# Transposing the inner layers of two routed expert blocks together, in three pieces

## The chip, the cores and the metric

The kernel runs on one core of a Trainium2 chip. A core has a matrix engine (TensorE, PE in the profile; its weight loads are shown apart as PEld), a vector engine (VectorE, DVE), a scalar engine (ScalarE, ACT), a general engine (GpSimd, POOL) and an engine that mostly issues transfers (SyncE, SP). Each has its own queue of instructions, taken in order; semaphores tie them together. Operands lie in an on-chip memory of 128 partitions; the matrix engine writes to a second, smaller one (PSUM), from which DVE and ACT copy. The metric is the device time of one execution, in microseconds (us). Twelve runs of the kernel before gave a median of 989.9 us, from 986.58 to 996.82 us.

## The reference

All arithmetic is in 32-bit floats. The input is x, 8 sequences of 256 tokens with 256 features (2048 tokens). Three residual layers follow one another:

```python
x = x + 0.5 * ffn(layernorm(x))      # mixture of experts
x = x + attention(layernorm(x))      # 16 heads, each query looks at its 32 best keys
x = x + 0.5 * ffn(layernorm(x))      # the same weights again

# ffn, for one token t with its 2 best of 8 experts:
scores = softmax(t @ gate_w)
routed = sum over the 2 experts e of
         scores[e] * (silu(t @ w_gate[e]) * (t @ w_up[e])) @ w_down[e]
shared = (silu(t @ sw_gate) * (t @ sw_up)) @ sw_down
out    = routed + shared
```

An expert's inner layer has 176 units, the shared one's 352. The change concerns the routed part only, which is computed in both feed-forward layers.

## The kernel before

**Routing.** Tokens are sorted by expert into blocks of 128 slots, so that all the tokens of one block use one expert. A block's tokens are fetched by an indirect transfer from a copy of the normalised tokens in DRAM, and its results are stored by an indirect transfer to `y_dram`; both are issued by POOL (L520 and L591). With 2048 tokens, two experts each and 8 experts, 37 blocks are always computed (`ND`), and two more only in a rare distribution, behind a branch (`rare`).

**A block.** Block b goes through these parts, in functions of these names:

- `fetch` (L520): 128 tokens come into tile `xs`, one token per partition.
- `turn` (L531, L533): two transposes on PE into PSUM (`px`), and one ACT copy into `xsT`.
- `widen` (L543 to L555): matmuls of `xsT` with the expert's gate and up weights give `pgu` (2 x 176 columns); ACT takes the silu (`sl`, L553), DVE multiplies it with the other half, and the inner layer `h` (128 tokens x 176 units, L555) is done. In the first pass a weight load for the attention is issued behind it.
- `turn_hidden` (L563, L565): the 176 units must come to the partitions for the next matmul. They are cut into two halves of 88: two PE transposes of 128 x 88 go into PSUM (`ph`), and one DVE copy of 88 partitions x 256 brings both to `hT`.
- `narrow` (L571 to L591): two accumulating matmuls over 88 units each, with 256 columns of `w_down`, give `py`. DVE works out the token's weight `ws` (L580), ACT multiplies (`y`, L589), POOL stores.

A matmul in 32-bit floats shows as two records in the profile, a transpose as one.

**Order.** `routed` runs over steps. In step s, PE does `widen(s)`, `turn(s+2)`, `turn_hidden(s-2)` and `narrow(s-4)`, so that each part was prepared one or more steps ago by ACT or DVE. A scheduler puts the instructions of each engine in order by their dependencies; PE keeps the order of the steps. PSUM has two buffers of each kind: `pgu`, `px`, `ph` and `py` can each be at most two blocks ahead of the engine that empties them. In SBUF, `xs` has 13 buffers (8 fetches are issued ahead), `xsT`, `h` and `hT` have 4 each and `y` has 8. POOL's queue holds fetches and stores alternately.

**Weights.** The eight experts' weights lie in one tile `wall`, a row of columns per expert; the two halves of `w_down` lie in partitions 0 to 87 in two column ranges. The expert for a block is chosen at run time by a column offset held in a register of PE (`locate`). The loads are issued by SP (L121) in the first layer's normalisation.

**Around it.** Ahead of the blocks stand the layer norm, the shared expert's first half and the routing; after them the shared expert of the remaining seven tiles, and then, in the first pass, the attention, in the second, the sum with the stored results (`yg`, L638; DVE L644) and the output.

Of the kernel before, what the change touches and what calls it, by code (L numbers as in the profile page):

```python
# [8 lines left out]
F32 = mybir.dt.float32  # L9
# [3 lines left out]
ALU = mybir.AluOpType  # L13
AX = mybir.AxisListType

P = 128
# [7 lines left out]
def macaron_kernel(  # L24
# [19 lines left out]
    nc = tc.nc  # L44

    B, S, D = x_in.shape
    NT = B * S // P
    KD = D // P
# [5 lines left out]
    E, _, HE = w_gate.shape  # L54
    HS = sw_gate.shape[1]
    K = 2
    assert E == 8 and HS == 2 * HE and HE % 2 == 0
    HH = HE // 2
    NSC = (HS + P - 1) // P


# [1 line left out]
    ND = (NT * P * K) // P + E // 2 + 1  # L63
# [18 lines left out]
    psum = ctx.enter_context(tc.tile_pool(name="psum", bufs=2, space=bass.MemoryType.PSUM))  # L82
# [12 lines left out]
    wall = wts.tile([P, E, EW], F32, name="wall")  # L95
# [24 lines left out]
    def later(loads, out, in_, queue=nc.sync):  # L120
        loads.append(lambda: queue.dma_start(out=out, in_=in_))  # L121

    for k in range(KD):
        for j, w in ((0, w_gate), (1, w_up)):
            c0 = (2 * k + j) * HE
# [4 lines left out]
            )  # L130
    for c in range(2):
        c0 = 2 * KD * HE + c * D
        later(
            expert_loads,
            wall[0:HH, :, c0 : c0 + D],
            w_down[:, c * HH : (c + 1) * HH, :].rearrange("e h d -> h e d"),
        )
    later(attn_loads, wi_sb[:, :, HI, :], wk_idx.rearrange("(k p) d -> p k d", p=P))
    later(attn_loads, wk_sb, wk.rearrange("(k p) d -> p k d", p=P))
# [18 lines left out]
    ident = const.tile([P, P], F32, name="ident")  # L158
# [287 lines left out]
    def ffn(n, pool, block_pool, ahead):  # L446
# [65 lines left out]
            nc.vector.scalar_tensor_tensor(x[:, i, :], po, 0.5, x[:, i, :], ALU.mult, ALU.add)  # L512

        w = wall.rearrange("p e c -> p (e c)")
        xs, xsT, hT, turned, c0 = {}, {}, {}, {}, {}

        def fetch(b, slot_pool):

            xs[b] = slot_pool.tile([P, DR], F32, tag="xs", name=f"xs_{n}_{b}", bufs=XB + XH)
            nc.gpsimd.indirect_dma_start(  # L520
                out=xs[b],
                out_offset=None,
                in_=xn_dram,
                in_offset=bass.IndirectOffsetOnAxis(ap=token[:, b : b + 1], axis=0),
            )

        def turn(b):

            px = psum.tile([P, KD, P], F32, tag="B", name=f"px_{n}_{b}")
            for k in range(KD):  # L530
                nc.tensor.transpose(px[:, k, :], xs[b][:, k * P : (k + 1) * P], ident)  # L531
            xsT[b] = block_pool.tile([P, KD, P], F32, tag="xsT", name=f"xsT_{n}_{b}", bufs=4)
            nc.scalar.copy(xsT[b], px)  # L533

        def locate(b):

            c0[b] = nc.tensor.value_load(cols[0:1, b : b + 1], min_val=0, max_val=(E - 1) * EW)

        def widen(b):

            pgu = psum.tile([P, 2, HE], F32, tag="A", name=f"pgu_{n}_{b}")
            for k in range(KD):
                nc.tensor.matmul(  # L543
                    pgu,
                    xsT[b][:, k, :],
                    w[:, bass.ds(c0[b] + 2 * k * HE, 2 * HE)],
                    start=(k == 0),
                    stop=(k == KD - 1),
                )
            if b + 1 < ND:  # L550
                locate(b + 1)
            sl = block_pool.tile([P, HE], F32, tag="sl", name=f"sl_{n}_{b}", bufs=3)
            nc.scalar.activation(sl, pgu[:, 0, :], AF.Silu)  # L553
            h = block_pool.tile([P, HE], F32, tag="h", name=f"h_{n}_{b}", bufs=4)
            scaled = nc.vector.tensor_tensor(h, sl, pgu[:, 1, :], ALU.mult)  # L555
            if attn_loads:
                behind(attn_loads.pop(0)(), scaled, "spread over the blocks")
            return h

        def turn_hidden(b, h):  # L560
            ph = psum.tile([HH, 2, P], F32, tag="C", name=f"ph_{n}_{b}")
            for c in range(2):
                nc.tensor.transpose(ph[:, c, :], h[:, c * HH : (c + 1) * HH], ident)  # L563
            hT[b] = block_pool.tile([HH, 2, P], F32, tag="hT", name=f"hT_{n}_{b}", bufs=4)
            turned[b] = nc.vector.tensor_copy(hT[b], ph)  # L565

        def narrow(b, slot_pool):

            py = psum.tile([P, D], F32, tag="D", name=f"py_{n}_{b}")
            for c in range(2):  # L570
                nc.tensor.matmul(  # L571
                    py,
                    hT[b][:, c, :],
                    w[0:HH, bass.ds(c0[b] + 2 * KD * HE + c * D, D)],
                    start=(c == 0),
                    stop=(c == 1),
                )
            ws = block_pool.tile([P, 1], F32, tag="ws", name=f"ws_{n}_{b}", bufs=4)
            with tc.issue_after(turned[b].ins):
                nc.vector.scalar_tensor_tensor(  # L580
                    ws,
                    xs[b][:, D + 1 : D + 2],
                    choice[:, b : b + 1],
                    xs[b][:, D : D + 1],
                    ALU.mult,
                    ALU.add,
                )
            y = slot_pool.tile([P, D], F32, tag="y", name=f"y_{n}_{b}", bufs=SB)
            nc.scalar.mul(y, py, ws)  # L589

            stored = nc.gpsimd.indirect_dma_start(  # L591
                out=y_dram,
                out_offset=bass.IndirectOffsetOnAxis(ap=dest[:, b : b + 1], axis=0),
                in_=y,
                in_offset=None,
            ).ins
            tc.declare_no_dep(stored, group=f"y_{n}", reason="rows that differ")
            tc.add_to_no_dep_group(f"y_{n}", stored)

        def routed(slot_pool):  # L600


            for b in range(XB):
                fetch(b, slot_pool)
            locate(0)
            turn(0)
            turn(1)
            h = {}
            for b in range(ND + 4):
                if b < ND:  # L610
                    h[b] = widen(b)
                if b + 2 < ND:
                    turn(b + 2)
                if 2 <= b < ND + 2:
                    turn_hidden(b - 2, h[b - 2])
                if b >= 4:
                    narrow(b - 4, slot_pool)
                if b + XB < ND:
                    fetch(b + XB, slot_pool)

        def rare(count, slot_pool):

            with tc.If(count > ND):
                for b in range(ND, NB):
                    fetch(b, slot_pool)
                    locate(b)
                    turn(b)
                    turn_hidden(b, widen(b))
                    narrow(b, slot_pool)

        parts = y_dram[NT * P * K : 2 * NT * P * K, :].rearrange("(i p k) d -> p i k d", k=K, p=P)
# [60 lines left out]
    igroups, c0 = [], 0  # L692
# [477 lines left out]
```

## Time and profile before

| | |
|---|---|
| median of 12 runs | 989.9 us |
| profiled execution, its own time | 990.67 us |
| span of the profiled execution | 988.7 us |
| mean granted TensorE clock | 0.987 |
| PE busy | 929.9 us (94%) |
| DVE busy | 513.2 us (52%) |
| ACT busy | 403.8 us (41%) |
| POOL busy | 305.8 us (31%) |
| first block's first matmul, first pass / second pass | at 68.05 / 848.45 us |
| last block's last matmuls begin, first pass / second pass | at 178.06 / 958.81 us |

The span runs from the first instruction to the last. A group is named by its line, its engine and its tiles ("ph<-ident,h" is written by a transpose of `h`), with the number of its instructions, its busy time and the mean time of one. A matmul's time covers its way through the array, so that a following one begins before it ends; what a matmul costs in a stream is read from the distance between starts.

### The profile page before, as it was taken

How to read it: one execution, taken by the hardware profiler on the slowest of the kernel's cores; microseconds unless marked ns; L12 is line 12 of the kernel's file. 1: busy time of each engine (PE TensorE's matmuls, PEld its weight loads, DVE VectorE, ACT ScalarE, POOL GpSimd, SP SyncE). 2: the span in 40 equal slices, each digit the busy share in tenths (PEclk: the TensorE clock that was granted, in tenths of full speed). 3: DMA queues.
4: the chain of work that ended last, by engine and by line, in shares of the span. 5: the costliest groups of instructions: out<-in, count | busy, mean ns of one | idle time of the engine just before them, and what ended most of it. 6: DMA issues, size and time to landing. Idle time of an engine off the chain costs nothing. (4 is left out here: it accounts for less than half of the span.)

```text
span 988.7 us, 16072 instructions
## 1 busy us (share of the span) xinstructions
PE 929.9 (94%) x4412; PEld 740.6 (75%) x4412; DVE 513.2 (52%) x1986; ACT 403.8 (41%) x1297; POOL 305.8 (31%) x501
## 2 busy tenths in 40 slices
PE   6998989999999999999999999999988999798898
PEld 3665667689878888888888888888867667566675
DVE  5442233594757566475464665565566527222236
ACT  4422333234554445435435435435434442233331
POOL 2035664300132232222222223223234400566640
PEclk9997999999999999999999999999999999999899
DMA  9324532342152433333243243233244610222217
GB/s 304 91 55 134 179 115 76 112 141 78 45 169 79 131 120 102 99 127 114 75 139 114 88 140 106 98 111 113 100 123 138 202 38 7 76 86 88 89 63 262
DMA packets 124158, 111.98 MB, mean 113 GB/s; under 512 B 32326, under 2 KB 106022, under 8 KB 124070
## 3 DMA queue, kind: packets, MB, share of 16 engines
q1 hardware_dynamic: 107078, 63.30, 22.3%
q0 software_dynamic: 14272, 45.18, 13.1%
q10 hardware_dynamic: 2720, 2.47, 0.8%
q8 instruction: 38, 0.62, 0.3%
q14 instruction: 50, 0.41, 0.1%
HBM read 63.97 MB, written 46.92 MB: 112 GB/s over the span
## 5 line engine op out<-in xcount | busy, mean ns | idle before, releaser
L945 POOL TENSOR_TENSOR s<-s,rden 128x512 f32<-128x512 f32 (+1 forms) x60 | 87.8, 1464 | 180.8 <-DVE rden L944 176.4
L543 PE MATMUL pgu<-wall,xsT 128*128 x296 | 106.1, 482 | 19.8 <-ACT xsT L533 10.5
L520 POOL DMA_INDIRECT xs<-xn_dram,token x74 | 71.3, 963 | 163.3 <-DVE dest L425 114.0
L935 ACT ACTIVATE s<-s,anm 128x32 f32<-128x32 f32 (+1 forms) x240 | 96.5, 404 | 54.1 <-DVE anm L931 19.1
L997 PE MATMUL pwo<-wo_sb,oT 128*128 128x256 f32 x512 | 116.9, 380 | 1.4 <-ACT oT L978 1.4
L676 PE MATMUL pqT<-xnT,wq_sb 128*128 128x256 f32 x512 | 116.7, 379 | 0.7 <-ACT qT L726 0.7
L997 PEld LDWEIGHTS pwo<-wo_sb,oT 128*128 128x128 f32 x512 | 96.4, 190 | 26.8 <-issue 9.1
L676 PEld LDWEIGHTS pqT<-xnT,wq_sb 128*128 128x128 f32 x512 | 96.8, 190 | 13.2 <-ACT qT L726 1.1
L676 PE MATMUL pqi<-xnT,wi_sb 128*128 128x224 f32 x512 | 103.3, 353 | 0.0
L555 DVE TENSOR_TENSOR h<-sl,pgu 128x176 f32<-128x176 f32 x74 | 24.9, 337 | 137.7 <-ACT sl L553 94.9
L676 PEld LDWEIGHTS pqi<-xnT,wi_sb 128*128 128x128 f32 x512 | 95.7, 190 | 0.8
L911 PE MATMUL ps<-kT,qT 128*128 128x160 f32 (+7 forms) x512 | 86.0, 310 | 7.7 <-DVE amx L920 4.6
L911 PEld LDWEIGHTS ps<-kT,qT 128*128 128x128 f32 x512 | 75.5, 191 | 21.3 <-ACT r L815 9.5
L543 PEld LDWEIGHTS pgu<-wall,xsT 128*128 128x128 f32 x296 | 56.5, 195 | 44.5 <-ACT xsT L533 16.6
L971 PE MATMUL pav<-s,v 128*128 128x512 f32 x180 | 87.9, 592 | 0.0
L591 POOL DMA_INDIRECT y_dram<-y,dest x74 | 71.8, 971 | 50.4 <-ACT y L589 28.7
L571 PE MATMUL py<-wall,hT 88*128 x296 | 78.3, 390 | 8.3 <-ACT y L589 8.3
L952 DVE STREAM_TRANSPOSE sq<-s 128x512 f32<-128x512 f32 (+1 forms) x60 | 58.5, 975 | 52.0 <-POOL s L945 52.0
L920 DVE CUSTOM_DVE_ANT_0 s<-ps,bias 128x32 f32<-128x32 f32 (+1 forms) x240 | 61.8, 300 | 42.4 <-PE ps L911 23.0
L800 DVE SCALAR_TENSOR_TENSOR acc<-r,iwp,acc 128x96 f32<-128x96 f32 x168 | 74.9, 499 | 13.7 <-ACT r L815 13.7
L978 ACT COPY oT<-pav 128x512 f32<-128x512 f32 x64 | 37.3, 583 | 69.7 <-PE pav L971 69.4
L589 ACT ACTIVATE y<-py,ws 128x256 f32<-128x256 f32 x74 | 35.3, 478 | 72.5 <-PE py L571 37.6
(171 smaller groups left out, 1450.8 us busy)
## 6 DMA issues: line engine op xcount, KB each, us to landing
s<-sq_dram SPq DMA_DIRECT2D x360, 64.0 KB
sq_dram<-sq POOLq DMA_DIRECT2D x32, 512.0 KB
sq_dram<-sq POOLq DMA_DIRECT2D x32, 256.0 KB
yg<-y_dram SPq DMA_DIRECT2D x18, 256.0 KB
xn_dram<-xn SPq DMA_DIRECT2D x32, 128.0 KB
yg<-y_dram SPq DMA_DIRECT2D x7, 512.0 KB
acc_dram<-acc SPq DMA_DIRECT2D x8, 368.0 KB
wi_sb<-in_L_attn_wq_idx_dram SPq DMA_DIRECT2D x8, 256.0 KB
```

The source lines that it names most:

```text
L520: nc.gpsimd.indirect_dma_start(out=xs[b], out_offset=None, in_=xn_dram, in_offset=bass.IndirectOffsetOnAxis(ap=token[:, b : b + 1], axis=0),)
L543: nc.tensor.matmul(pgu, xsT[b][:, k, :], w[:, bass.ds(c0[b] + 2 * k * HE, 2 * HE)], start=(k == 0), stop=(k == KD - 1),)
L571: nc.tensor.matmul(py, hT[b][:, c, :], w[0:HH, bass.ds(c0[b] + 2 * KD * HE + c * D, D)], start=(c == 0), stop=(c == 1),)
L591: stored = nc.gpsimd.indirect_dma_start(out=y_dram, out_offset=bass.IndirectOffsetOnAxis(ap=dest[:, b : b + 1], axis=0), in_=y, in_offset= ...
L676: nc.tensor.matmul(ps[:, j, :], weights(k, h0 + hh + j), xnT[:, k, b * S + skip : (b + 1) * S], start=(k == 0), stop=(k == KD - 1),)
L800: nc.vector.scalar_tensor_tensor(acc[:, cols], r, iw, acc[:, cols], ALU.mult, ALU.add)
L911: nc.tensor.matmul(ps[:, c0 - first : c0 - first + n], qT[:, t * NQ + q].rearrange("p h k -> p (h k)"), kT[:, 0:n], start=True, stop=True,)
L920: nc.vector.tensor_tensor_reduce(out=s[:, q, 0:n], in0=ps[:, c0 - first : c0 - first + n], in1=bias[t][:, c0 : c0 + n], scale=1.0, scalar= ...
L935: nc.scalar.activation(scores, scores, AF.Exp, bias=nm[:, q : q + 1], scale=SCALE, accum_out=den[:, q : q + 1],)
L945: nc.gpsimd.tensor_tensor(s, s, rden.unsqueeze(2).to_broadcast([P, NQ, ns]), ALU.mult)
L971: nc.tensor.matmul(po.rearrange("p h r -> p (h r)"), v[:, c, 0:HD], pT[:, c].rearrange("p h r -> p (h r)"), start=(c == 0), stop=(c == t),)
L997: nc.tensor.matmul(po, oT[:, h, :], wo_sb[:, w0 + h, :], start=(h == 0), stop=(h == HW - 1),)
```

## The change

The inner layer is cut into 112 and 64 units instead of 88 and 88, and two blocks share one tile `h` of 352 columns: first the 112 and the 64 of the even block, then the 64 and the 112 of the odd one, so that the two pieces of 64 lie side by side. The even block's multiplication stays one DVE instruction, the odd one's becomes two. Every second step, three transposes serve two blocks: one of 112 columns for each, and one of 128 columns that holds both pieces of 64; they land in partitions 0 to 63 and 64 to 127. DVE then copies each block's 112 partitions and its 64 partitions, 128 columns each, four copies for two blocks, where there were two of 256 columns. The second matmul of `narrow` works on 64 partitions. `narrow` runs five steps after `widen` instead of four; the tile `h` has 3 buffers of double width, `hT` 5. The 37th block has no partner and is turned alone, with two transposes. The load of `w_down` is cut at 112.

```diff
-    HH = HE // 2
+    HT = P // 2
+    HM = HE - HT
...
-            wall[0:HH, :, c0 : c0 + D],
-            w_down[:, c * HH : (c + 1) * HH, :].rearrange("e h d -> h e d"),
+            wall[0:n, :, c0 : c0 + D],
+            w_down[:, h0 : h0 + n, :].rearrange("e h d -> h e d"),
...
-            h = block_pool.tile([P, HE], F32, tag="h", name=f"h_{n}_{b}", bufs=4)
-            scaled = nc.vector.tensor_tensor(h, sl, pgu[:, 1, :], ALU.mult)
+            if j == 0:
+                hs[b] = hs[b + 1] = block_pool.tile(
+                    [P, 2 * HE], F32, tag="h", name=f"h_{n}_{b}", bufs=3
+                )
+            for lo, hi, to in ((0, HE, 0),) if j == 0 else ((HM, HE, HE), (0, HM, HE + HT)):
+                scaled = nc.vector.tensor_tensor(
+                    hs[b][:, to : to + hi - lo], sl[:, lo:hi], pgu[:, 1, lo:hi], ALU.mult
+                )
...
-            ph = psum.tile([HH, 2, P], F32, tag="C", name=f"ph_{n}_{b}")
-            for c in range(2):
-                nc.tensor.transpose(ph[:, c, :], h[:, c * HH : (c + 1) * HH], ident)
-            hT[b] = block_pool.tile([HH, 2, P], F32, tag="hT", name=f"hT_{n}_{b}", bufs=4)
-            turned[b] = nc.vector.tensor_copy(hT[b], ph)
+            b, m = blocks[0], len(blocks)
+            ph = psum.tile([P, 3, P], F32, tag="C", name=f"ph_{n}_{b}")
+            for j in range(m):
+                to = j * (HE + HT)
+                nc.tensor.transpose(ph[0:HM, j, :], hs[b][:, to : to + HM], ident)
+            nc.tensor.transpose(ph[0 : m * HT, 2, :], hs[b][:, HM : HM + m * HT], ident)
+            for j in range(m):
+                hT[b + j] = block_pool.tile([P, 2, P], F32, tag="hT", name=f"hT_{n}_{b + j}", bufs=5)
+                nc.vector.tensor_copy(hT[b + j][0:HM, 0, :], ph[0:HM, j, :])
+                turned[b + j] = nc.vector.tensor_copy(
+                    hT[b + j][0:HT, 1, :], ph[j * HT : (j + 1) * HT, 2, :]
+                )
...
             for c in range(2):
+                rows = (HM, HT)[c]
                 nc.tensor.matmul(
                     py,
-                    hT[b][:, c, :],
-                    w[0:HH, bass.ds(c0[b] + 2 * KD * HE + c * D, D)],
+                    hT[b][0:rows, c, :],
+                    w[0:rows, bass.ds(c0[b] + 2 * KD * HE + c * D, D)],
...
-            for b in range(ND + 4):
+            for b in range(ND + 5):
                 if b < ND:
-                    h[b] = widen(b)
+                    widen(b, b % 2)
                 if b + 2 < ND:
                     turn(b + 2)
-                if 2 <= b < ND + 2:
-                    turn_hidden(b - 2, h[b - 2])
-                if b >= 4:
-                    narrow(b - 4, slot_pool)
+                if b % 2 and b >= 3 and b - 3 < ND:
+                    turn_hidden(range(b - 3, min(b - 1, ND)))
+                if b >= 5:
+                    narrow(b - 5, slot_pool)
```

More of the change, by code (lines that the diff above doesn't have):

```diff
@@ L56, in macaron_kernel @@
     K = 2
-    assert E == 8 and HS == 2 * HE and HE % 2 == 0
-    HH = HE // 2
+    assert E == 8 and HS == 2 * HE and P // 2 < HE <= P + P // 2
+    HT = P // 2
+    HM = HE - HT
     NSC = (HS + P - 1) // P
@@ L132, in macaron_kernel @@
         c0 = 2 * KD * HE + c * D
+        h0, n = c * HM, (HM, HT)[c]
         later(
             expert_loads,
-            wall[0:HH, :, c0 : c0 + D],
-            w_down[:, c * HH : (c + 1) * HH, :].rearrange("e h d -> h e d"),
+            wall[0:n, :, c0 : c0 + D],
+            w_down[:, h0 : h0 + n, :].rearrange("e h d -> h e d"),
         )
@@ L514, in ffn @@
         w = wall.rearrange("p e c -> p (e c)")
-        xs, xsT, hT, turned, c0 = {}, {}, {}, {}, {}
+        xs, xsT, hs, hT, turned, c0 = {}, {}, {}, {}, {}, {}
         def fetch(b, slot_pool):
@@ L537, in locate, with widen @@
             c0[b] = nc.tensor.value_load(cols[0:1, b : b + 1], min_val=0, max_val=(E - 1) * EW)
-        def widen(b):
+        def widen(b, j):
             pgu = psum.tile([P, 2, HE], F32, tag="A", name=f"pgu_{n}_{b}")
@@ L553, in widen, with turn_hidden @@
             nc.scalar.activation(sl, pgu[:, 0, :], AF.Silu)
-            h = block_pool.tile([P, HE], F32, tag="h", name=f"h_{n}_{b}", bufs=4)
-            scaled = nc.vector.tensor_tensor(h, sl, pgu[:, 1, :], ALU.mult)
+            if j == 0:
[6 more added lines that the diff above has]
+                )
             if attn_loads:
                 behind(attn_loads.pop(0)(), scaled, "spread over the blocks")
-            return h
-        def turn_hidden(b, h):
-            ph = psum.tile([HH, 2, P], F32, tag="C", name=f"ph_{n}_{b}")
-            for c in range(2):
-                nc.tensor.transpose(ph[:, c, :], h[:, c * HH : (c + 1) * HH], ident)
-            hT[b] = block_pool.tile([HH, 2, P], F32, tag="hT", name=f"hT_{n}_{b}", bufs=4)
-            turned[b] = nc.vector.tensor_copy(hT[b], ph)
+        def turn_hidden(blocks):
+            b, m = blocks[0], len(blocks)
[10 more added lines that the diff above has]
+                )
         def narrow(b, slot_pool):
@@ L607, in routed @@
             turn(1)
-            h = {}
-            for b in range(ND + 4):
+            for b in range(ND + 5):
                 if b < ND:
-                    h[b] = widen(b)
+                    widen(b, b % 2)
                 if b + 2 < ND:
                     turn(b + 2)
-                if 2 <= b < ND + 2:
-                    turn_hidden(b - 2, h[b - 2])
-                if b >= 4:
-                    narrow(b - 4, slot_pool)
+                if b % 2 and b >= 3 and b - 3 < ND:
+                    turn_hidden(range(b - 3, min(b - 1, ND)))
+                if b >= 5:
+                    narrow(b - 5, slot_pool)
                 if b + XB < ND:
@@ L627, in rare @@
                     turn(b)
-                    turn_hidden(b, widen(b))
+                    widen(b, 0)
+                    turn_hidden([b])
                     narrow(b, slot_pool)
```

## The prediction

> **What bounds the kernel now.** I read the page first, for the shares of the engines, then PE's instructions in order of time through both stretches of blocks, then POOL's, and last the groups by line. The page:
>
> ```profile
> PE 929.9 (94%) x4412; PEld 740.6 (75%) x4412; DVE 513.2 (52%) x1986; ACT 403.8 (41%) x1297; POOL 305.8 (31%) x501
> PE   6998989999999999999999999999988999798898
> ```
>
> PE is the bound nearly everywhere: a slice is 24.7 us, and the first pass of the blocks lies in slices 3 to 8, the second in 35 to 39. What PE saves or loses in the blocks is handed on, since it is busy behind both stretches too. So the blocks' own steps decide. PE in the first pass, columns start, time, instruction, and in brackets the idle time before it with what ended it:
>
> ```profile
> 104.47 1.35 PE L543 MATMUL pgu<-wall,xsT 128*128 x4
> 105.66 0.38 PE L531 MATMUL px<-ident,xs 128*128 128x128 f32 x2
> 105.87 0.38 PE L563 MATMUL ph<-ident,h 128*88 128x128 f32 x2
> 106.09 1.03 PE L571 MATMUL py<-wall,hT 88*128 x4
> 106.96 1.35 PE L543 MATMUL pgu<-wall,xsT 128*128 x4
> 108.14 0.38 PE L531 MATMUL px<-ident,xs 128*128 128x128 f32 x2
> ...
> 108.58 1.03 PE L571 MATMUL py<-wall,hT 88*128 x4
> 111.03 1.45 PE L543 MATMUL pgu<-wall,xsT 128*128 x4 [1.42 <-issue]
> ...
> 126.13 1.13 PE L571 MATMUL py<-wall,hT 88*128 x4 [1.81 <-ACT y L589]
> ...
> 157.19 1.45 PE L543 MATMUL pgu<-wall,xsT 128*128 x4 [1.12 <-ACT xsT L533]
> ```
>
> An undisturbed step takes 106.96 - 104.47 = 2.49 us without a gap: pgu 1.19, px 0.21, ph 0.22, py 0.87 by the distances of starts. One transpose costs 0.108 us. But PE also waits, and for ACT: from the fifth step's pgu (86.52) to the 29th's (157.19) 24 steps take 70.7 us where 24 x 2.49 = 59.8 would do, so 10.9 us are lost; in the second pass (864.65 to 938.04) it is 13.6 us. From step 29 on there is no wait in either pass. What differs then is POOL:
>
> ```profile
> 106.88 0.98 POOL L591 DMA_INDIRECT y_dram<-y,dest  x1 [0.30 <-issue]
> 108.16 0.97 POOL L520 DMA_INDIRECT xs<-xn_dram,token  x1 [0.31 <-issue]
> 109.44 0.98 POOL L591 DMA_INDIRECT y_dram<-y,dest  x1 [0.30 <-issue]
> 113.36 0.97 POOL L520 DMA_INDIRECT xs<-xn_dram,token  x1 [2.94 <-PE ph L563]
> ...
> 165.70 0.96 POOL L591 DMA_INDIRECT y_dram<-y,dest  x1 [1.53 <-ACT y L589]
> ```
>
> While fetches and stores are both issued, a block costs POOL 2 x 1.28 = 2.56 us, more than PE's 2.49; it runs in dense rows of about eight, and ACT falls behind in them. After the last fetch (151.82) POOL idles 1.53 us per store and ACT is on time. Why ACT falls behind in POOL's dense rows the trace does not tell; that it does is enough here.
>
> **The change, part by part.** The rows for its costs, five groups by line (busy us, mean ns of one | idle before) and one instruction from the order of time:
>
> ```profile
> L571 PE MATMUL py<-wall,hT 88*128 x296 | 78.3, 390 | 8.3 <-ACT y L589 8.3
> L565 DVE COPY hT<-ph 88x256 f32<-88x256 f32 x74 | 30.8, 416 | 22.7 <-PE ph L563 10.8 <-remote 7.0 <-PE px L531 3.5
> L555 DVE TENSOR_TENSOR h<-sl,pgu 128x176 f32<-128x176 f32 x74 | 24.9, 337 | 137.7 <-ACT sl L553 94.9 <-issue 35.4 <-ACT y L589 6.9
> L507 PE MATMUL po<-wsd_sb,gT 96*128 96x256 f32 x64 | 19.1, 379 | 0.0
> L580 DVE SCALAR_TENSOR_TENSOR ws<-xs,choice 128x1 f32<-128x1 f32 x74 | 15.3, 207 | 0.0
> 60.80 0.24 DVE L407 COPY tk_f<-tk 128x78 f32<-128x78 f32 x1 [1.99 <-PE tk L399]
> ```
>
> *Transposes.* 37 blocks make 18 pairs and a single. A pair saves one transpose: 18 x 0.108 = 1.94 us a pass, 3.9 us in all, if all of it gets through. The pieces still stream 128 columns each, so their width saves nothing.
>
> *The result's matmuls.* Count and columns (256) stay. With 88, 96 or 128 partitions the time is the same (379 ns, L571 median and L507), so the uneven cut as such is free. But the built program gives the matmul over 64 partitions an array tile of 64 rows x 128 columns, where every matmul of before has 128 x 128 (the smallest height in any row is 88). So PE changes the tile's height twice per block, 148 times in all, and no row of before shows what that costs. From below: nothing, as changing from multiplying to transposing and back leaves no gap (106.09 follows 105.87 by two transposes of 0.108). From above: the array runs empty first and then starts cold. A py record lasts 379 ns and four of them 1.03 us, so they start (1.03 - 0.379) / 3 = 0.217 us apart; 0.162 us of each lies under the next one. A chain that starts after a wait takes 1.45 instead of 1.35 us (111.03 against 106.96), 0.10 us. Together 0.26 us a change. I take 0.162 us, the overlap alone: a change of height is one that no overlapping pair in this trace makes, while weights are loaded ahead everywhere. In the 13 blocks per pass whose results lie where PE never waits this gets through: 26 x 0.162 = 4.2 us. In the other 24 it is 48 x 0.162 = 7.8 us beside 10.9 and 13.6 us of waits for ACT: a slower PE eats into those waits, but POOL, paced by PE, is also stretched. Between none and all I take half, 3.9 us.
>
> [...] With the gapless rows as the rule the sum would be the 3.9 us gain, with a drain as long as the overlap it is the loss below.
>
> *DVE.* A pair took 2 x (337 + 414 + 206) = 1914 ns. Now: one multiplication of 337, two of 64 and 112 columns (between 206 at 1 column and 337 at 176, say 250 and 290), four copies of 128 columns (between 240 at 78 and 414 at 256, say 290), two ws: 2.45 us of about 4.9. Both ws of a pair now stand behind its four copies, so the even block's xs is freed a step later; its 13 buffers leave POOL's fetch nine steps of lead. The hT of a pair's even block is ready some 1 us later within its step than before, still two steps ahead of `narrow`. Covered, zero; if DVE were late it would show as a wait of py for hT, which before held PE only once (81.68, 3.7 us).
>
> *Five steps instead of four.* PE's total is the same; the first result stands one step later and five instead of three results follow one another at the end without a pgu between. POOL needs 1.27 us per store there and PE 0.87 per result, so the last store lands 0 to 0.8 us later; the second pass's sum waits for it: 0.4 us, once. ACT, SP and POOL have the same instructions, in the same order.
>
> *Load of w_down.* The same bytes, issued at 19.7 us, first used at 85: free.
>
> *Sum.* Per pass -1.9 + 4.2 + 3.9 = +6.2; twice and 0.4: +12.8 us on the execution's own 990.67: 1003.5. That execution stood 0.8 us above the median, so 1002.7.
>
> **The rivals.**
>
> 1. *The height change is free, and PE's saving gets through.* The gapless rows speak for it. 990.67 - 3.9 - 0.8 = 986.0, faster. It decides below 3.9 / 148 = 26 ns a change.
> 2. *Free, but the saving is lost in the waits for ACT.* Where POOL's 2.56 us set the pace, a faster PE only waits longer; only the 6 pairs outside steps 5 to 28 count: 6 x 0.108 x 2 = 1.3 us, 988.6: no difference.
> 3. *Drain and cold start, nothing hidden.* 148 x 0.26 = 38.5, less 3.9: 1024.
> 4. *DVE turns late.* The 0.54 us more per pair fall into some six waits a pass: 6.5 less 3.9, 992.5. Against it: half of DVE's time is free.
>
> That no transpose is saved can be left out: the order of the changed kernel's instructions has three for a pair.
>
> **How the numbers follow.** Forecast 0.45, its own range 994 (all of the middle stretch hidden: -3.9 + 8.4 + 0.4) to 1010 (none); rivals 0.25, 0.13, 0.10 and 0.07. About 0.3% (3 us) is what can be told from no change. Faster takes most of rival 1: 0.22; the same, the rest of it, most of rival 2 and a sliver of 4: 0.18; slower 0.60. The range from 985.5 to 1016 leaves out rival 3 and the tails of rival 1 and the forecast.
>
> **What would show it.** Starts in an undisturbed pair of steps: 4.87 us for two if the change of height is free, about 5.5 by the forecast, with the gap on both sides of the second matmul of py. The ph group should have 2 x (18 x 3 + 2) = 112 records instead of 148. PE's waits for ACT between steps 5 and 29 should shrink if they are eaten into. It would be wrong if py's four records still fit into 1.03 us, or if hT from DVE is what py waits for.

## The result and the profile after

The changed kernel takes 1004.4 us in the median of 15 runs (999.76 to 1011.25), the kernel before 991.55 us in 62 runs beside it. The ratio is 1.0138, with a 95% interval from 1.012 to 1.0157: the change makes the kernel 13.7 us slower (the medians lie 12.9 us apart). The forecast was 1002.7 us, in a range of 985.5 to 1016. The profiled execution has a span of 1003.3 us, against 988.7.

The page of the changed kernel, its totals and PE's busy time in 40 slices:

```profile
PE 952.1 (95%) x4376; PEld 726.4 (72%) x4376; DVE 521.7 (52%) x2096; ACT 404.4 (40%) x1297; POOL 305.8 (30%) x501
PE   6997979999999999999999999999989999798998
```

PE has 36 instructions fewer (the transposes saved) and is busy 22.2 us longer. Where this comes from is seen in PE's instructions in order of time, in a stretch of the first pass where PE waits for nobody (start, time, instruction):

```profile
162.41 1.45 PE L545 MATMUL pgu<-wall,xsT 128*128 x4
163.70 0.38 PE L533 MATMUL px<-ident,xs 128*128 128x128 f32 x2
163.92 1.22 PE L588 MATMUL py<-wall,hT 112*128 x4
165.07 1.45 PE L545 MATMUL pgu<-wall,xsT 128*128 x4
166.36 0.38 PE L533 MATMUL px<-ident,xs 128*128 128x128 f32 x2
166.58 0.38 PE L574 MATMUL ph<-ident,h 128*112 128x128 f32 x2
166.80 0.27 PE L575 MATMUL ph<-ident,h 128*128 128x128 f32 x1
166.91 1.22 PE L588 MATMUL py<-wall,hT 112*128 x4
168.06 0.56 PE L545 MATMUL pgu<-wall,xsT 128*128 x1
```

A pair of steps takes 168.06 - 162.41 = 5.65 us, with three transposes instead of four; two steps of before took 4.98. The four records of py take 1.22 instead of 1.03 us; pgu behind them starts 1.15 instead of 0.87 us after their start and takes 1.45 instead of 1.35. Without any extra cost the pair would take 4.98 - 0.108 = 4.87; the rest, 0.78 us, is four changes of the tile's height at 0.195 us.

The weight loads of the same stretch, first of the changed kernel, then of the kernel before:

```profile
164.45 0.29 PEld L588 LDWEIGHTS py<-wall,hT 64*128 64x128 f32 x2 [0.33 <-issue]
165.07 0.89 PEld L545 LDWEIGHTS pgu<-wall,xsT 128*128 128x128 f32 x4 [0.33 <-issue]
```

```profile
163.78 0.73 PEld L571 LDWEIGHTS py<-wall,hT 88*128 88x128 f32 x4
164.54 1.00 PEld L543 LDWEIGHTS pgu<-wall,xsT 128*128 128x128 f32 x4
```

Before, the loads for pgu follow those for py and begin 0.21 us ahead of the first matmul (at 164.75). After, the loads for the 64 rows and those for pgu each begin 0.33 us after the load before them has ended, and pgu's load and its first matmul carry the same start, 165.07: behind these changes of height nothing is loaded ahead. The changed kernel's groups by line (busy us, mean ns of one | idle before):

```profile
L545 PE MATMUL pgu<-wall,xsT 128*128 x296 | 112.8, 506 | 22.6 <-ACT xsT L535 14.1 <-DVE h L562 4.7 <-ACT sl L555 2.0
L588 PE MATMUL py<-wall,hT 112*128 (+1 forms) x296 | 92.2, 411 | 0.4 <-issue 0.3
```

py rose from 78.3 to 92.2 us, but its idle time fell from 8.3 to 0.4: PE no longer waits for `y` (pgu's idle time rose, from 19.8 to 22.6 us). From the first pgu of a pass to the shared expert's next matmul, the two stretches of blocks took 121.3 and 119.9 us (66.99 to 188.29, 856.49 to 976.38), 241.2 together; before it was 112.6 and 113.0, 225.6. So the blocks took 15.6 us more, all of the loss. Had each step run at its undisturbed spacing, before would have needed 74 x 2.49 = 184.3 us and after 2 x (18 x 5.65 + 2.88) = 209.2. What is left, 41.3 us before and 32.0 after, is lost to waits: PE's idle time in the stretches (28.4 and 22.8 us) and slower matmuls right behind long waits. So the full price is 24.9 us, and 9.3 are given back by waits. All of that lies in steps 5 to 29, where the lost time fell from 24.5 to 14.8 us; the other steps lost 16.8 and 17.2.

### The profile page after: what moved, and what is told of

Its sections match the earlier page's. It is cut to its first block, busy times and chain, and to the rows that moved or that the text cites. A ratio compares the mean times of both kernels' runs of the same rounds, so it can differ in the third digit from the quotient of the medians.

```text
span 1003.3 us, 16017 instructions
## 1 busy us (share of the span) xinstructions
PE 952.1 (95%) x4376; PEld 726.4 (72%) x4376; DVE 521.7 (52%) x2096; ACT 404.4 (40%) x1297; POOL 305.8 (30%) x501
## 5 line engine op out<-in xcount | busy, mean ns | idle before, releaser
L545 PE MATMUL pgu<-wall,xsT 128*128 x296 | 112.8, 506 | 22.6 <-ACT xsT L535 14.1
L562 DVE TENSOR_TENSOR h<-sl,pgu 128x176 f32<-128x176 f32 (+2 forms) x110 | 27.3, 276 | 152.1 <-ACT sl L555 111.2
L545 PEld LDWEIGHTS pgu<-wall,xsT 128*128 128x128 f32 x296 | 53.0, 199 | 62.2 <-issue 23.6
L588 PE MATMUL py<-wall,hT 112*128 (+1 forms) x296 | 92.2, 411 | 0.4 <-issue 0.3
L817 DVE SCALAR_TENSOR_TENSOR acc<-r,iwp,acc 128x96 f32<-128x96 f32 x168 | 74.9, 500 | 12.8 <-ACT r L832 12.7
L588 PEld LDWEIGHTS py<-wall,hT 112*128 112x128 f32 (+1 forms) x296 | 44.9, 190 | 28.5 <-issue 22.1
```

What stands on the lines that cost most here:

```text
L545: nc.tensor.matmul(pgu, xsT[b][:, k, :], w[:, bass.ds(c0[b] + 2 * k * HE, 2 * HE)], start=(k == 0), stop=(k == KD - 1),)
L588: nc.tensor.matmul(py, hT[b][0:rows, c, :], w[0:rows, bass.ds(c0[b] + 2 * KD * HE + c * D, D)], start=(c == 0), stop=(c == 1),)
L817: nc.vector.scalar_tensor_tensor(acc[:, cols], r, iw, acc[:, cols], ALU.mult, ALU.add)
```

## The experiments

The theory ("height"): each of the 148 changes between an array tile of 128 rows and one of 64 costs PE 0.195 us, and waits for ACT hide a part. The profile shows the rows that a matmul uses, not the tile; what the runs can show is which neighbours in rows (64, 88, 96, 112, 128) cost something. Rivals: DVE is late; the pairing or the longer distance disturbs the blocks; the 64-row matmul itself is slow, whatever stands beside it.

The runs came in three sets, each on a chip of its own with its own runs of the kernel before: medians 988.6, 990.7 and 950.5 us. The third chip is 4% faster with the same kernel; why that matters is told below. "Stretches" are the two stretches of blocks in the one profiled execution, "lost" is what they hold beyond the undisturbed steps.

| kernel | set | ratio to before (95%) | undisturbed pair of steps | stretches | lost |
|---|---|---|---|---|---|
| before | (first profile) | 1 | 4.98 | 225.6 | 41.3 |
| changed | (first profile) | 1.0138 (1.012, 1.0157) | 5.65 | 241.2 | 32.0 |
| tall_all | 1 | 1.0028 (0.9999, 1.0058) | 4.87 | 219.3 | 38.2 |
| tall_early | 1 | 1.0167 (1.0126, 1.0208) | 4.87, then 5.65 | 229.6 | 39.2 |
| tall_late | 1 | 1.0144 (1.0098, 1.019) | 5.65, then 4.87 | 223.5 | 23.7 |
| uneven | 1 | 1.0087 (1.0052, 1.0123) | 5.76 | 235.4 | 22.2 |
| tall_free | 2 | 0.996 (0.9936, 0.9984) | 4.87 | 219.2 | 38.1 |
| mirror | 2 | 1.0075 (1.0047, 1.0102) | 5.26 | 234.2 | 39.1 |
| split | 2 | 0.9979 (0.9954, 1.0003) | 4.98 | 223.8 | 39.5 |
| before5 | 2 | 0.9963 (0.9939, 0.9987) | 4.98 | 218.4 | 34.1 |
| tall_free4 | 3 | 0.9946 (0.9929, 0.9963) | 4.87 | 180.1 | 0 |
| after_4 | 3 | 1.0219 (1.0194, 1.0243) | 5.65 | 207.8 | 0 |
| tall_free6 | 3 | 0.998 (0.9969, 0.9992) | 4.87 | 180.1 | 0 |
| before6 | 3 | 1.0022 (1.0008, 1.0036) | 4.98 | 183.3 | 0 |

On the third chip the stretches come out 1.0 to 1.4 us shorter than all steps at their spacing, mostly because the first two blocks are turned ahead of the first pgu (four transposes a pass, 0.9 us in all); lost is put at 0.

### No change of height: tall_all

The second result matmul of a paired block runs over 96 rows; the 32 rows added to `w_down`'s second range are zero and add nothing to the sum.

```diff
+    HL96 = 96
+    nc.gpsimd.memset(wall[HT:HL96, :, 2 * KD * HE + D :], 0.0)
...
+                r = HL96 if j == 0 and tall(b + j, m) else HT
                 turned[b + j] = nc.vector.tensor_copy(
-                    hT[b + j][0:HT, 1, :], ph[j * HT : (j + 1) * HT, 2, :]
+                    hT[b + j][0:r, 1, :], ph[j * HT : j * HT + r, 2, :]
                 )
+                if j == 1 and tall(b + j, m):
+                    turned[b + j] = nc.vector.tensor_copy(
+                        hT[b + j][HT:HL96, 1, :], ph[0 : HL96 - HT, 2, :]
+                    )
...
-                rows = (HM, HT)[c]
+                rows = (HM, rows_of[b])[c]
```

> The pairing, the three transposes and the five steps stay; only the second result matmul of a paired block runs over 96 rows (the 32 added rows of w_down's second range are zeros), so that its array tile is 128 x 128 like all others. DVE gets more work, not less: one more copy of 32 rows per pair.
> Theory 'height' (a change of the tile's height costs about 0.19 us, 148 times, some 10 us of it hidden in waits for ACT): the loss goes entirely. Two undisturbed steps take 4.87 us, four records of py 1.03 us again, and the time is that of before less 3.9 us (ratio 0.996) if the saved transposes get through, less 1.3 us (0.999) if the waits for ACT swallow what lies in steps 5 to 28.
> Rival 'DVE' (copies and multiplications too late for PE): the loss stays, 1.014 or more, as DVE has 18 more copies a pass.
> Rival 'pairing and distance' (the transposes of two blocks in one step, results five steps on, disturb the order): the loss stays, about 1.014.

Measured: 990.79 us, 1.0028 (0.9999 to 1.0058). The pair of steps falls to 4.87 us and py's four records to 1.03, with DVE doing more than in the changed kernel. So neither DVE nor the pairing makes the loss; with the height constant it is gone. The 0.996 to 0.999 expected was just missed, and the stretches of blocks (219.3 against 225.6) say that the kernel should have gained. Most of the gain went into the start: the memset had been put first on POOL's queue, 1.80 us ahead of the identity matrix, PE's first transposes began at 10.90 instead of 9.15 us, and the first pgu at 71.79 instead of 68.05. The part between the two stretches was 1.8 us longer as well (669.6 against 667.8), within what it varies from kernel to kernel (665.4 to 672.5).

### The zeros written later: tall_free

The edit, against tall_all:

```diff
-    nc.gpsimd.memset(wall[HT:HL96, :, 2 * KD * HE + D :], 0.0)
...
     nc.gpsimd.memset(inner[:, :, 0:1], 0.0)
+    nc.gpsimd.memset(wall[HT:HL96, :, 2 * KD * HE + D :], 0.0)
```

> The kernel whose paired blocks all run over 96 rows, with the zeros written at the end of POOL's work at the start instead of ahead of it. There the memset (1.80 us) stood ahead of the identity matrix, the first transposes began at 10.90 instead of 9.15 us and the first pgu at 71.8 instead of 67.0 to 68.1.
> Theory 'height and a late start': the stretches of blocks took 219.3 us against 225.6 of before, so only the start hides the gain: 3.7 to 4.8 us less than the first version, ratio to before 0.994 to 0.999.
> Rival 'the start is caught up with before the blocks': no difference to the first version, 1.003.
> Rival 'the pairing costs something besides the height': 1.003 or more, with the stretches of blocks no shorter than 225 us.

Measured: 986.88 us, 0.996 (0.9936 to 0.9984), as the theory had it; the blocks took 219.2 us again, the first pgu began at 69.09. PE's order of time in an undisturbed pair of this kernel:

```profile
165.23 1.35 PE L547 MATMUL pgu<-wall,xsT 128*128 x4
166.41 0.38 PE L535 MATMUL px<-ident,xs 128*128 128x128 f32 x2
166.63 0.38 PE L580 MATMUL ph<-ident,h 128*112 128x128 f32 x2
166.85 0.27 PE L581 MATMUL ph<-ident,h 128*128 128x128 f32 x1
166.96 1.03 PE L600 MATMUL py<-wall,hT 112*128 x4
167.83 1.35 PE L547 MATMUL pgu<-wall,xsT 128*128 x4
```

py is back at 1.03 us and pgu at 1.35, 0.87 us behind it: the prices of before, with 112 and 96 rows. The distance to the changed kernel, 1.0138 - 0.996 = 0.0178 or 17.6 us, is what 144 changes cost in time (the single last block of each pass keeps its two); in full they are 144 x 0.195 = 28.1.

### The uneven cut alone: uneven

The kernel before with pieces of 112 and 64 rows; no pairs, two transposes a block, four steps.

```diff
-            for c in range(2):
-                nc.tensor.transpose(ph[:, c, :], h[:, c * HH : (c + 1) * HH], ident)
+            nc.tensor.transpose(ph[0:HM, 0, :], h[:, 0:HM], ident)
+            nc.tensor.transpose(ph[:, 1, :], h[:, HE - P :], ident)
...
-            turned[b] = nc.vector.tensor_copy(hT[b], ph)
+            nc.vector.tensor_copy(hT[b][0:HM, 0, :], ph[0:HM, 0, :])
+            turned[b] = nc.vector.tensor_copy(hT[b][0:HT, 1, :], ph[HT:P, 1, :])
```

> The kernel before with the uneven cut alone: 112 and 64 columns, the second result matmul over 64 rows; no pairs, two transposes a block as before, results four steps on. One DVE copy more per block (as in the changed kernel).
> Theory 'height': 148 changes at 0.194 = 28.7 us less 10 to 14 us of waits: 15 to 19 us longer than before (1.015 to 1.019), an undisturbed step 2.88 us instead of 2.49, four records of py 1.22.
> Rival 'pairing and distance': as before, 1.000, since neither is in it.
> Rival 'DVE': up to the 1.014 of the changed kernel, with py waiting for hT in the trace.

Measured: 996.28 us, 1.0087 (1.0052 to 1.0123). The price is exactly the one expected; PE's order of time:

```profile
162.29 1.45 PE L545 MATMUL pgu<-wall,xsT 128*128 x4
163.58 0.38 PE L533 MATMUL px<-ident,xs 128*128 128x128 f32 x2
...
164.02 1.22 PE L574 MATMUL py<-wall,hT 112*128 x4
165.17 1.45 PE L545 MATMUL pgu<-wall,xsT 128*128 x4
```

A step is 165.17 - 162.29 = 2.88 us, 0.39 more than 2.49, for two changes; there is no pair in this kernel, so the price belongs to the cut. But the total was missed, 7.7 us instead of 15 to 19: of 28.9 us only 9.8 appear in the stretches, since the lost time fell from 41.3 to 22.2. How much the waits hide was underrated here.

### Half as many changes, the same matmuls: mirror

The two results of a pair stand side by side, the second with its halves reversed: rows 112, 64, 64, 112.

```diff
-        def narrow(b, slot_pool):
+        def narrow(b, slot_pool, order=(0, 1)):
...
-            for c in range(2):
+            for c in order:
...
-                if b >= 5:
+                if b % 2 and b >= 5:
                     narrow(b - 5, slot_pool)
+                    if b - 4 < ND:
+                        narrow(b - 4, slot_pool, (1, 0))
```

> The changed kernel, with the two results of a pair in one step next to each other and the second one's halves in the reverse order: 112, 64, 64, 112 rows. The 64-row matmuls stay 74 per execution and their weight loads too, but there are 76 changes of height instead of 148. Results of an odd block come one step sooner.
> Theory 'a change of height costs 0.195 us': an undisturbed pair of steps takes 4.87 + 2 x 0.195 = 5.26 us (5.65 in the changed kernel), in all 14 us less than the changed kernel in full, 5 to 8 us by the share that waits swallow: 1.006 to 1.009 to before.
> Rival 'it is the 64-row matmul or its weight load that is slow, whatever stands beside it': 5.65 us a pair, 1.014.

Measured: 999.22 us, 1.0075 (1.0047 to 1.0102), within the theory's 1.006 to 1.009 and clear of the rival's 1.014. PE's order of time, then the weight loads, which show where the price sits:

```profile
161.54 1.35 PE L545 MATMUL pgu<-wall,xsT 128*128 x4
...
164.68 2.28 PE L588 MATMUL py<-wall,hT 112*128 x8
166.80 1.35 PE L545 MATMUL pgu<-wall,xsT 128*128 x4
```

```profile
164.57 0.30 PEld L588 LDWEIGHTS py<-wall,hT 112*128 112x128 f32 x2
165.20 0.73 PEld L588 LDWEIGHTS py<-wall,hT 64*128 64x128 f32 x4 [0.33 <-DVE h L562]
166.26 0.30 PEld L588 LDWEIGHTS py<-wall,hT 112*128 112x128 f32 x2 [0.33 <-issue]
166.58 1.00 PEld L545 LDWEIGHTS pgu<-wall,xsT 128*128 128x128 f32 x4
```

Four loads of 64 rows run into each other, 0.73 us for four as with 88 rows, and the loads of pgu follow those of 112 rows without a gap. The idle 0.33 us stands only where the height changes, twice a pair. The pair of steps takes 166.80 - 161.54 = 5.26 us, 2 x 0.195 above 4.87, and pgu behind 112 rows is back at 1.35 us. So the price is that of the change, not of a 64-row matmul or of its load.

### Where the changes stand: tall_early and tall_late

```diff
-            return m == 2 and True
+            return m == 2 and b < 24
```

(and `b >= 24` for tall_late, with the memset still at the front in both)

> As the kernel whose paired blocks all run over 96 rows, but only in blocks 0 to 23 of each pass; the last 13 blocks keep the 64-row matmul, 52 changes of height in all, where PE hardly waits.
> Theory 'height': these get through in full, 52 x 0.194 = 10.1 us over the kernel without changes (ratio to before 1.006 to 1.009).
> Rival 'all changes cost the same everywhere, nothing is hidden': the share 26 / 74 of the whole loss, 35% of it.
> Rivals 'DVE' and 'pairing and distance': no difference to the kernel without changes or to the changed kernel, whatever those are.

> The other half: 96 rows only in blocks 24 to 35 of each pass; the first 24 blocks and the single last one keep the 64-row matmul, 100 changes of height, 96 of them where PE waits for ACT.
> Theory 'height, partly hidden': 100 x 0.194 = 19.4 us, of which the shrunken waits for ACT give back about 9.7: 9.7 us over the kernel without changes (ratio to before 1.006 to 1.009), so that a change here is worth about half of one in the last blocks.
> Rival 'nothing is hidden': 19.4 us, 1.016 to 1.019, more than the changed kernel itself.
> Rival 'all hidden': the same time as the kernel without changes.

Measured: tall_early 1.0167 (1.0126 to 1.0208), tall_late 1.0144 (1.0098 to 1.019), from four runs each. tall_all itself has four changes left, those of the single last blocks, so tall_early has 48 more than it and tall_late 96 more. Against tall_all the stretches grew by some 10 us in tall_early, all of its 48 x 0.195 = 9.4, and by 4.2 in tall_late, whose 96 changes cost 18.7 in full: PE's waits fell there (lost 38.2 to 23.7). That speaks for "paid in full where PE doesn't wait, hidden in part where it does". The times are less kind: 11.7 us and 9.4 us by the medians, where 10.1 and 9.7 had been expected, and the two together are more than the 17.6 us that all changes cost. The profiled executions were also the fastest of their four (998.14 and 994.44 us, beside medians of 1002.47 and 1000.17), so the stretches show less than an average execution pays. The intervals are 8 to 9 us wide. That a part is hidden is shown by uneven (19.1 of 28.9 us); its share isn't settled by these two.

### DVE alone and the distance alone: split and before5

```diff
-            turned[b] = nc.vector.tensor_copy(hT[b], ph)
+            for c in range(2):
+                turned[b] = nc.vector.tensor_copy(hT[b][:, c, :], ph[:, c, :])
```

> The kernel before, only the copy of hT in two of 128 columns (about 284 ns each) instead of one of 256 (414): DVE gets 0.15 us more a block, no other engine changes.
> Theory 'DVE is covered': 1.000, an undisturbed step still 2.49 us.
> Rival 'DVE late': the two passes lose up to 74 x 0.15 = 11 us, 1.005 to 1.011.

```diff
-            for b in range(ND + 4):
+            for b in range(ND + 5):
...
-                if b >= 4:
-                    narrow(b - 4, slot_pool)
+                if b >= 5:
+                    narrow(b - 5, slot_pool)
```

> The kernel before, only results five steps on instead of four (a fifth buffer for hT).
> Theory: 0 to 0.8 us a pass for the last stores, 1.000 to 1.001.
> Rival 'the distance disturbs the blocks': a larger part of the 13 us of the changed kernel, above 1.005, with longer waits of PE in the blocks.

Measured: split 0.9979 (0.9954 to 1.0003). Two copies of 280 ns instead of one of 416 cost nothing; DVE is covered. before5 0.9963 (0.9939 to 0.9987): the longer distance, put down at no gain at all, is worth 3.7 us. The waits that it takes are those of py, group of before5 by line:

```profile
L571 PE MATMUL py<-wall,hT 88*128 x296 | 76.3, 383 | 2.9 <-issue 1.4 <-ACT y L589 1.4
```

Before, py idled 8.3 us for `y`; here 2.9, of which 1.4 for `y`, and the lost time of the stretches falls from 41.3 to 34.1 us. Why `y` comes sooner isn't shown: the distance from one result to the next is the same with four steps and five. Nor does the shorter wait come with every kernel of five steps. In tall_free py waits longer than before, and it is pgu that waits less (15.0 us instead of 19.8):

```profile
L600 PE MATMUL py<-wall,hT 112*128 (+2 forms) x296 | 78.4, 390 | 11.6 <-ACT y L618 11.0 <-issue 0.6
```

tall_free is as fast as before5, which has no pairs (986.9 and 987.0 us). So beside five steps the pairs are worth nothing on this chip: the saved transposes, 3.9 us, are matched by 4.0 us more of lost time (38.1 against 34.1). That the 0.996 is the distance's doing is the plain reading, but pairs at four steps were not run on this chip.

### The same on a chip without these waits: tall_free4, after_4, tall_free6, before6

The edits are the distance of tall_free, of the changed kernel and of before5, set to four or six, for six with one more buffer of `hT` and of `xs`:

```diff
-    XH = 5
+    XH = 6
...
-            for b in range(ND + 5):
+            for b in range(ND + 6):
...
-                if b >= 5:
-                    narrow(b - 5, slot_pool)
+                if b >= 6:
+                    narrow(b - 6, slot_pool)
```

> Pairs with 96 rows and the zeros written late, but results four steps on, as in the kernel before: the pairing alone, without a change of height and without the longer distance.
> Theory 'the saved transposes are lost in the waits' (the version with five steps, 0.996, was no faster than the kernel before with five steps, 0.9963, so the distance made all of the gain): 0.999 to 1.001, and stretches of blocks near the 225.6 us of before.
> Rival 'the saving gets through and the distance is worth nothing with pairs': 0.996, stretches near 219 us.

> The changed kernel with results four steps on.
> Theory 'distance helps': 3 to 4 us longer than the changed kernel, 1.017 to 1.018 to before, with longer waits of py for ACT.
> Rival 'the slower steps leave the distance nothing to win': 1.014, as the changed kernel.
> Rival 'the distance is part of the loss': below 1.014.

> Pairs with 96 rows, zeros late, results six steps on, with one buffer more for hT and one more for xs (the fetches keep their lead).
> Theory 'the distance relieves the waits for ACT, and more of it relieves more': 1 to 3 us less than with five steps, 0.993 to 0.995.
> Rival 'five steps are enough, what is left are waits for xsT': 0.996.

> The kernel before with results six steps on, one buffer more for hT and for xs than with five.
> Theory 'more distance relieves more': 0.993 to 0.995.
> Rival 'five are enough': 0.996. Against the version with pairs and 96 rows at six steps it shows what the saved transposes are worth once the waits are shorter: 3.9 us if they get through, 0 if not.

The expectations came from the first two chips, and most were missed, because this chip has no waits in the blocks. The groups of py and pgu in before6, then in after_4:

```profile
L543 PE MATMUL pgu<-wall,xsT 128*128 x296 | 99.9, 459 | 0.2 <-ACT xsT L533 0.2
L571 PE MATMUL py<-wall,hT 88*128 x296 | 74.8, 379 | 0.0
```

```profile
L545 PE MATMUL pgu<-wall,xsT 128*128 x296 | 106.4, 482 | 0.2 <-ACT xsT L535 0.2
L588 PE MATMUL py<-wall,hT 112*128 (+1 forms) x296 | 90.7, 405 | 0.0
```

Of PE's 28.4 us of idle time in the stretches of the first profile none is left here (the 0.2 us lie ahead of the first pgu). All steps run at their spacing, and each edit shows at its full price in the stretches. tall_free4, the pairing without a change of height, 0.9946 (0.9929 to 0.9963): the saving gets through, 4.8 us in the medians (945.69 against 950.47). tall_free6 against before6, the same step at six, gives 3.0 us in the medians and 183.3 - 180.1 = 3.2 in the stretches, which is the 3.9 us of the sum less the four changes of height that are left (0.8). The changes of height, after_4 against tall_free4: stretches 207.8 - 180.1 = 27.7 us for 144 x 0.195 = 28.1, and 25.0 us in the medians; in the stretches nothing is hidden, as there is nothing to hide in. Six steps do not help where nothing waits: before6 1.0022, and tall_free6 3.8 us above tall_free4, though their stretches are equal (180.1); its time lies outside the blocks (first pgu at 70.71 against 68.47, 2.8 us more between the passes), and why is open. What four or five steps are worth to the changed kernel can't be read from after_4, as the changed kernel wasn't run on this chip.

tall_free4 beats the kernel before on the chip on which it ran, and after_4, the changed kernel with four steps, by 25 us. On the chips with waits it wasn't run; there tall_free beat the kernel before.

## Why the prediction was right

The time was 1.7 us above the forecast, and the term that carried the forecast, the change of the tile's height, is what the runs show. Its parts and two smaller terms were off. Step by step:

- **Transposes, -3.9 us.** Right as a price: 4.87 us a pair in tall_all, and 112 records of ph (74 + 36 + 2). Whether it gets through depends on the waits. With them it didn't (tall_free and before5 equal, which is rival 2's mechanism), without them it did (tall_free4, tall_free6).
- **Change of height, 0.162 us.** The cause was right, the size 0.033 too small: 0.195 in three kernels of different build, (5.65 - 4.87) / 4, (2.88 - 2.49) / 2 and (5.26 - 4.87) / 2. For 148 changes that is 28.9 us in full instead of 24.0. The lower bound, nothing, from the gapless rows of before, fell; the upper, 0.26, held. But the parts are not those that were chosen, the whole overlap and no cold start. In the changed kernel py's records end at 163.92 + 1.22 = 165.14 and pgu begins at 165.07, so 0.07 us of overlap remain; before it was 106.09 + 1.03 - 106.96 = 0.16. (The profile models these ends.) So 0.09 us of the overlap went, and the cold start, 0.10 us, which the prediction had named and left out, came on top: pgu takes 1.45 instead of 1.35 us. That 0.162 lies so near 0.195 is in part luck. The weight loads show where the price sits: those behind a change of height begin 0.33 us after the load before them has ended, and where the height stays, py's four follow one another without such a gap (0.73 us for four, over 88 rows in the kernel before and over 64 in mirror). What PE does in the 0.33 us isn't shown.
- **Half hidden in the middle steps.** The forecast let 16.2 of 24.0 us through, 68%. Of 28.1, 17.6 came through in time (63%) and 241.2 - 219.2 = 22.0 in the stretches (78%). As a size it held: in steps 5 to 29 the lost time fell by 9.7 us (24.5 to 14.8) where the forecast let 7.8 be hidden. But before5 loses only 19.6 us there, so half of that may be the distance's. The half was a guess between none and all, other kernels hid other shares (uneven 19.1 of 28.9), and what it leans on, the waits, belongs to the chip.
- **DVE, 0.** Right: split shows no cost, and py's weight loads wait for `hT` 0.7 us in all in the changed kernel. The wait of 3.7 us at 81.68 that the prediction gave as one of py for `hT` stands ahead of a pgu, which doesn't read `hT`.
- **Five steps, +0.4.** Wrong in sign on the chip with waits: -3.7 us (before5). The step costed the last stores and kept PE's total, and left out that the distance could change the waits for ACT. In before5 py's wait for `y` fell from 8.3 to 1.4 us; by what path is open.
- **Sum.** The forecast's terms were 16.2 for the height, +0.4 for the distance and -3.9 for the transposes, 12.8 with rounding. The runs: 17.6 for the height (the changed kernel against tall_free), -3.7 for the distance (before5), nothing of the 3.9 saved (tall_free against before5). Together that is 13.9 beside the 13.7 of the result, but this agreement proves nothing: the three differences lead from the kernel before over before5 and tall_free to the changed kernel, and add up to the result however it is divided. The near hit is in part luck: a distance that was not counted and a saving that was lost cancel, 4.1 us against 3.9.

Of the rivals, the first (free change) fell, with 0.195 us against its 26 ns; the third (38.5 us, nothing hidden) took the upper bound; its clause "nothing hidden" is what the third chip does, where after_4 lost 20.3 us. The fourth (DVE) fell with split and with tall_all, which gives DVE more work and loses nothing in the blocks.

One argument of the prediction fell as well, that POOL's dense rows of fetches and stores are where ACT falls behind. On the third chip the pauses are as short and ACT is on time. ACT in the kernel before (first profile), then ACT and POOL in before6:

```profile
103.64 0.37 ACT L533 COPY xsT<-px 128x256 f32<-128x256 f32 x1
106.30 0.47 ACT L589 ACTIVATE y<-py,ws 128x256 f32<-128x256 f32 x1 [2.29 <-PE ph L563]
109.23 0.32 ACT L553 ACTIVATE sl<-pgu 128x176 f32<-128x176 f32 x1 [2.46 <-PE ph L563]
```

```profile
90.14 0.47 ACT L589 ACTIVATE y<-py,ws 128x256 f32<-128x256 f32 x1 [0.71 <-PE py L571]
91.33 0.32 ACT L553 ACTIVATE sl<-pgu 128x176 f32<-128x176 f32 x1 [0.71 <-PE pgu L543]
...
92.63 0.47 ACT L589 ACTIVATE y<-py,ws 128x256 f32<-128x256 f32 x1 [0.71 <-PE py L571]
```

```profile
90.48 0.98 POOL L591 DMA_INDIRECT y_dram<-y,dest  x1 [0.30 <-issue]
91.76 0.97 POOL L520 DMA_INDIRECT xs<-xn_dram,token  x1 [0.30 <-PE ph L563]
93.03 0.98 POOL L591 DMA_INDIRECT y_dram<-y,dest  x1 [0.30 <-issue]
```

POOL's pause is 0.30 us in both; ACT idles an even 0.71 us here and 2.29 and 2.46 there. So POOL's dense rows alone do not make ACT late. What makes it late on the other chips remains open.

## What to carry to other kernels

A matmul over 64 rows between matmuls over 112 or 128 cost PE 0.195 us twice, once for each change of the array tile's height, and each is more than the 0.108 us that a saved transpose gives back. Look at the tile shape that the built program gives each matmul; pad the short one with zero rows until its tile is the others' (96 rows were enough here), or put the short ones side by side so that the height changes half as often. And before a saving on an engine is counted, ask whether the engine waits there: pairing without a change of height was worth nothing beside before5 on a chip with waits, and its full price on one without.

## What was not expected of the hardware

- The same kernel took 990.7 us on one chip and 950.5 on another. The 40 us are the time lost in the blocks: 41.3 us in the first profile, and on the third chip stretches of 183.3 us against 225.6. (That is before6; the kernel before was timed there but not profiled.) POOL's indirect transfers take 0.97 us on both. Why PE waits on one chip and not on the other is open.
- Two long waits cost more than themselves. In the kernel before PE waited 3.84 us ahead of 857.43, and the next pgu took 2.50 us; in the changed kernel it waited 5.84 us, and its next pgu took 2.71 instead of 1.45 us. Windows behind this wait (the column ahead of the DMA share is the granted clock):

```profile
80.50:83.00 2.50, 2.41 (x4) 1.40 (x5) 1.54 (x8) 0.52 (x3) 0.04 (x1) 0.50 0.07 7
83.00:85.50 2.50, 2.50 (x8) 1.64 (x7) 0.34 (x1) 0.69 (x2) 1.84 (x2) 0.61 0.32 83
85.50:90.00 4.50, 4.50 (x21) 2.70 (x20) 1.88 (x9) 1.75 (x6) 1.55 (x2) 1.00 0.47 150
```

The granted clock is 0.50, then 0.61, then 1.00. This pgu and its px took 2.93 us (80.59 to 83.52) where 1.51 is usual, and the next pgu 2.07 instead of 1.45: some 2 us on top of the wait. In the kernel before the granted clock was 0.56 behind its wait of 3.84 us (857.40 to 859.90), and 1.00 behind the wait of 1.42 us ahead of 111.03 (111.00 to 113.00).

- A memset of 1.80 us put first on POOL moved PE's first transposes by 1.75 us and the first block by 3.7 us. In tall_free it stands later, at 4.08 us, but still ahead of other opening work of POOL, and the first transposes begin at 10.22 instead of 9.15 us. At the first block (69.09 against 68.05) that isn't clear of what the start varies in kernels without a memset (66.99 to 69.53).

- Only the height was seen to cost. The single last block's second transpose loads 64 columns over all 128 rows (128*64), and the starts around it stay 0.11 us apart, as between equal transposes; tall_free4:

```profile
156.30 0.27 PE L580 MATMUL ph<-ident,h 128*112 128x128 f32 x1
156.41 0.27 PE L581 MATMUL ph<-ident,h 128*64 128x128 f32 x1
156.52 2.09 PE L600 MATMUL py<-wall,hT 112*128 x8
```

There are only two such transposes in an execution.
